# Pairwise outer products with batch norm: longer store runs and a rebuilt head, on one core

## Chip, cores, metric

The kernel runs on one core of one Trainium2 chip. The metric is the device time of one execution in microseconds, median of several.

## The reference

```python
# xi, xj: (1024, 39, 16); rows, cols: the 741 pairs r > c of 39 fields; W: (1, 16, 16)
cross = xj[:, rows, :, None] * xi[:, cols, None, :]
mean = jnp.mean(cross, axis=(0, 2, 3), keepdims=True)
var = jnp.mean(jnp.square(cross - mean), axis=(0, 2, 3), keepdims=True)
normed = (cross - mean) * jax.lax.rsqrt(var + 1e-5)
normed = normed * gamma[None, :, None, None] + beta[None, :, None, None]
out = normed[:, :, None, :, :] * W[None, None, :, :, :]      # 1024 x 1 x 741 x 16 x 16, fp32
```

The output is 777 MB, the inputs 5 MB. The mean and variance of each pair come from small moments of xi and xj (the head); then the kernel makes the output tile by tile. A tile is one row r (its r columns, each 256 numbers or 1 KB) for two of the eight batch indices t of each partition.

## The kernel before

```python
T = 2
WHOLE, LONG = 19, 28              # rows in one piece, in two; longer in four
FIRST_PIECES = (0, 3, 9, 19)
POOL_I, POOL_SHARE = 4, 0.13
ROW_GROUPS = ((19, 20), (15, 19), (20, 25), (25, 32), (1, 15), (32, 39))
# ... cut: pools, tiles, views
    half = T * (F - 1)
    mid = (F - 1) // 2
    tiles = [(mid, t0, t0 // T * half // 2) for t0 in range(0, NT, T)]
    slot = 0
    for r in range(mid + 1, F):
        for t0 in range(0, NT, T):
            tiles.append((r, t0, slot * half))
            if r < F - 1:
                tiles.append((F - 1 - r, t0, slot * half + T * r))
            slot ^= 1
# ... cut
    def products(n):              # every i fills all columns of the tile for one t
        xs = xs_of.pop(n)
        for t in range(T):
            for i in range(E):
                product(n, nc.scalar if i < E - POOL_I else nc.gpsimd, t, i, xs[:, t])

    def store(n, c0, c1):
        r, t0, _ = tiles[n]
        n0 = first[r]

        step = 1 if r > LONG and c1 == r else T
        for t in range(0, T, step):
            nc.sync.dma_start(
                out_v[:, t0 + t : t0 + t + step, (n0 + c0) * EE : (n0 + c1) * EE],
                view(n)[:, t : t + step, c0:c1, :].rearrange("p t n e -> p t (n e)"),
            )
# ... cut: affine, weigh (tiles 0 and 1)
    def bounds(r):
        if r <= WHOLE:
            return (0, r)
        if r <= LONG:
            return (0, r // 2, r)
        return (0, r // 5, r // 2, r - r // 5, r)

    def finish(n):

        r = tiles[n][0]
        n0 = first[r]
        y = view(n)
        split = r - int(r * POOL_SHARE + 0.5)
        for c in range(split, r):
            nc.gpsimd.tensor_scalar(
                y[:, :, c, :], y[:, :, c, :], t_sb[:, n0 + c : n0 + c + 1], 1.0, ALU.add, ALU.mult
            )
        if split < r:
            nc.gpsimd.tensor_tensor(
                y[:, :, split:r, :],
                y[:, :, split:r, :],
                w_sb.unsqueeze(1).to_broadcast([P, T, r - split, EE]),
                ALU.mult,
            )
        for c0, c1 in zip(bounds(r), bounds(r)[1:]):
            for c in range(c0, min(c1, split)):
                stt(
                    y[:, :, c, :],
                    y[:, :, c, :],
                    t_sb[:, n0 + c : n0 + c + 1],
                    w_dve.to_broadcast([P, T, EE]),
                    ALU.add,
                    ALU.mult,
                )
            store(n, c0, c1)
# ... cut: loads (x in four pieces of two t; W from GpSimd, gamma and beta into scratch),
#     then the statistics on two t at a time
        raw0 = raw_products(0, nc.scalar, range(32))
        raw1 = raw_products(1, nc.scalar, range(20))
        sums(0)
        emit(raw0, 8)
        nc.scalar.copy(w_dve, w_sb)
        for t in range(T):
            nc.tensor.matmul(
                ps_s[:, 0 : 2 * F], ones, total[:, t], start=t == 0, stop=t == T - 1
            )
        for t in range(T):
            nc.tensor.matmul(
                ps_r[0:F, 0:1], total[:, t, 0:F], ones[:, 0:1], start=t == 0, stop=t == T - 1
            )
# ... cut: shift, deviations (GpSimd), squares (ACT), moments and means (DVE), gram (PE)
        for to, acc in zip((g1, g2, g3), ps_g):
            nc.scalar.activation(to, acc[0:F, 0 : 2 * F + 1], AF.Copy, scale=1.0 / NB)
# ... cut: 14 DVE operations from these copies to var, all in SBUF; reciprocal, root on ACT,
#     five more operations to scale and shift (stq)
        def spread(r0, r1):
            n0, n1 = first[r0], first[r1 - 1] + r1 - 1
            ps = psx.tile([P, 512], F32, tag="ps", name="ps")
            ps_v = ps[:, 0 : 2 * (n1 - n0)].rearrange("p (x n) -> p x n", x=2)
            for r in range(r0, r1):
                nc.tensor.matmul(
                    ps_v[:, :, first[r] - n0 : first[r] - n0 + r],
                    pick[:, r, :],
                    stq[:, :, 0:r],
                    start=True,
                    stop=True,
                )
            nc.vector.tensor_tensor(
                st_sb[:, :, n0:n1],
                ps_v,
                gb_all[:, 0:1, n0:n1].to_broadcast([P, 2, n1 - n0]),
                ALU.mult,
            )
            nc.vector.tensor_add(st_sb[:, 1, n0:n1], st_sb[:, 1, n0:n1], gb_all[:, 1, n0:n1])

        spread(*ROW_GROUPS[0])
        affine(0)
        weigh(0, FIRST_PIECES)
        scale_xi(2)
        spread(*ROW_GROUPS[1])
        spread(*ROW_GROUPS[2])
        affine(1)
        weigh(1, bounds(tiles[1][0]))
        for group in ROW_GROUPS[3:]:
            spread(*group)

        for n in range(1, len(tiles)):
            if n == 1:
                products(2)
                scale_xi(3)
                continue
            if n + 2 < len(tiles):
                scale_xi(n + 2)
            finish(n)
            if n + 1 < len(tiles):
                products(n + 1)
```

Rows r and 38 - r form a pair that fills one half of the output buffer; the two halves alternate. ACT and GpSimd (POOL) make the products of a tile, DVE (and POOL for the last 13% of the columns) adds the shift and multiplies by W, SP issues the stores.

Terms used below. A *piece* is the part of a row's columns that leaves as one run for each batch index; a *packet* is what one of the 16 DMA engines moves at a time, here one run. A store *lands* when its last packet is written; the *lag* is how much later that is than the time at which as many bytes had left on average. A *hole* is time in which DMA engines stand idle, averaged over the 16 unless the text says that all rest. *Two pairs* is the time in which two pairs of rows are stored, some 47 us: the *loop through the buffer*, from the products of a tile to the landing that frees its place, has to fit into it. In the head, *raw products* are those of tiles 0 and 1, made before the statistics are known; the *affine* then applies scale and shift to them, *weighing* multiplies by W, and *spreading* copies the row factors (scale and shift of each pair) to all partitions by PE.

Of the kernel before, what the change touches and what calls it, by code (L numbers as in the profile page):

```python
# [7 lines left out]
F32 = mybir.dt.float32  # L8
# [4 lines left out]
BN_EPS = 1e-5  # L13
# [3 lines left out]

WHOLE = 19
LONG = 28
FIRST_PIECES = (0, 3, 9, 19)  # L20

POOL_I = 4
POOL_SHARE = 0.13

ROW_GROUPS = ((19, 20), (15, 19), (20, 25), (25, 32), (1, 15), (32, 39))


@with_exitstack
def tile_pair_outer_batchnorm(
# [40 lines left out]
    psp = ctx.enter_context(tc.tile_pool(name="ps", bufs=1, space=bass.MemoryType.PSUM))  # L70
    psx = ctx.enter_context(tc.tile_pool(name="psx", bufs=2, space=bass.MemoryType.PSUM))
    xi_sb = cpool.tile([P, NT, F, E], F32, name="xi_sb")
# [34 lines left out]
    pick = scratch("rest", F, F, P)  # L107
    gb_all = scratch("rest", P, 2, NP)
    total = scratch("rest", P, NT, 2 * F)
# [3 lines left out]
    shift_r = scratch("rest", F, 1)  # L113
    g1, g2, g3 = (scratch("rest", F, 2 * F + 1) for _ in range(3))
    k, mean, q1, q2, var, rstd, inv = (scratch("rest", F, F) for _ in range(7))
    stq = scratch("rest", F, 2, F)
    ps_s = psp.tile([P, 512], F32, name="ps_s")
    ps_r = psp.tile([P, 512], F32, name="ps_r")
    ps_g = [psp.tile([P, 512], F32, name=f"ps_g{n}") for n in range(3)]
    stt = nc.vector.scalar_tensor_tensor  # L120
# [39 lines left out]
    def products(n):  # L160

        xs = xs_of.pop(n)
        for t in range(T):
            for i in range(E):
                product(n, nc.scalar if i < E - POOL_I else nc.gpsimd, t, i, xs[:, t])

    def store(n, c0, c1):
        r, t0, _ = tiles[n]
        n0 = first[r]

        step = 1 if r > LONG and c1 == r else T
        for t in range(0, T, step):
            nc.sync.dma_start(  # L173
                out_v[:, t0 + t : t0 + t + step, (n0 + c0) * EE : (n0 + c1) * EE],
                view(n)[:, t : t + step, c0:c1, :].rearrange("p t n e -> p t (n e)"),
            )
# [27 lines left out]
    def bounds(r):  # L204
        if r <= WHOLE:
            return (0, r)
        if r <= LONG:
            return (0, r // 2, r)
        return (0, r // 5, r // 2, r - r // 5, r)

# [29 lines left out]
    with tc.manual_schedule():  # L240
        for t0 in range(0, NT, T):
            nc.sync.dma_start(xj_sb[:, t0 : t0 + T], xj_v[:, t0 : t0 + T])
            nc.scalar.dma_start(xi_sb[:, t0 : t0 + T], xi_v[:, t0 : t0 + T])
        nc.gpsimd.dma_start(w_sb[:, 0, :], w.rearrange("o i j -> (o i j)").partition_broadcast(P))
        nc.sync.dma_start(gb_all[:, 0], gamma.partition_broadcast(P))
        nc.scalar.dma_start(gb_all[:, 1], beta.partition_broadcast(P))
        nc.gpsimd.memset(ones, 1.0)
        nc.gpsimd.memset(fb[:, :, 2 * F : 2 * F + 1], 1.0)

# [8 lines left out]

        k_s = 1.0 / (T * P * E)
        batches = range(0, NT, T)  # L260
        sources = (xj_sb, xi_sb)
# [3 lines left out]

        def sums(t0):
            for x in range(2):
                nc.vector.tensor_reduce(  # L268
                    total[:, t0 : t0 + T, part(x)], sources[x][:, t0 : t0 + T], AX.X, ALU.add
                )  # L270
# [10 lines left out]
        def square(n):  # L281

            nc.scalar.activation(devs[n % 7], devs[n % 7], AF.Square, scale=0.25)  # L283

# [6 lines left out]
        def means(n):  # L291
            t0, x = n // 2 * T, n % 2
            to = fb if x else fa
            stt(  # L294
                to[:, t0 : t0 + T, 0:F],
                total[:, t0 : t0 + T, part(x)],
                1.0 / E,
                ps_u[:, x : x + 1, :].to_broadcast([P, T, F]),
                ALU.mult,
                ALU.subtract,  # L300
            )
# [8 lines left out]
        raw0 = raw_products(0, nc.scalar, range(32))  # L310
        raw1 = raw_products(1, nc.scalar, range(20))
        sums(0)
        emit(raw0, 8)
        nc.scalar.copy(w_dve, w_sb)
        for t in range(T):
            nc.tensor.matmul(
                ps_s[:, 0 : 2 * F], ones, total[:, t], start=t == 0, stop=t == T - 1
            )
        for t in range(T):
            nc.tensor.matmul(  # L320
                ps_r[0:F, 0:1], total[:, t, 0:F], ones[:, 0:1], start=t == 0, stop=t == T - 1
            )

        nc.scalar.activation(
            shift.rearrange("p x f -> p (x f)"), ps_s[:, 0 : 2 * F], AF.Copy, scale=k_s
        )
        nc.scalar.activation(shift_r, ps_r[0:F, 0:1], AF.Copy, scale=k_s)  # L327
        ps_u = ps_s[:, 2 * F : 4 * F].rearrange("p (x f) -> p x f", x=2)
        nc.scalar.copy(ps_u, shift)
        sums(2)  # L330
        for n in range(7):
            deviation(n)
        for n in range(2 * NT // T):
            square(n)
            emit(raw0, 3)
            if n % 2 == 1 and n < 5:
                sums(n + 3)
            moments(n)
            if n == 0:
                deviation(7)  # L340
            means(n)
            if n % 2 == 1:
                gram(n // 2 * T)
        emit(raw_products(1, nc.gpsimd, range(20, 32)), 12)
        emit(raw1, 6)

# [3 lines left out]

        for to, acc in zip((g1, g2, g3), ps_g):
            nc.scalar.activation(to, acc[0:F, 0 : 2 * F + 1], AF.Copy, scale=1.0 / NB)
        e_ab, e_abb, e_a = g1[:, 0:F], g1[:, F : 2 * F], g1[:, 2 * F : 2 * F + 1]
        e_aab, e_aabb, e_aa = g2[:, 0:F], g2[:, F : 2 * F], g2[:, 2 * F : 2 * F + 1]
        e_b, e_bb = g3[:, 0:F], g3[:, F : 2 * F]
        u, v = shift_r, shift[0:F, 1, :]
        emit(raw1, 6)

        stt(q2, e_ab, u, e_aab, ALU.mult, ALU.add)
        stt(k, e_b, u, e_ab, ALU.mult, ALU.add)  # L360
        nc.vector.tensor_scalar_mul(q2, q2, 2.0)
        stt(k, v, e_a, k, ALU.mult, ALU.add)
        stt(q2, v, e_aa, q2, ALU.mult, ALU.add)
        stt(q1, e_bb, u, e_abb, ALU.mult, ALU.add)
        nc.vector.tensor_mul(q2, q2, v)
        nc.vector.tensor_add(q1, q1, e_abb)
        stt(mean, v, u, k, ALU.mult, ALU.add)
        stt(q1, q1, u, e_aabb, ALU.mult, ALU.add)
        nc.vector.tensor_mul(k, k, k)
        nc.vector.tensor_add(q1, q1, q2)  # L370
        nc.vector.tensor_sub(q1, q1, k)
        nc.vector.tensor_scalar(var, q1, 0.0, BN_EPS, ALU.max, ALU.add)


        nc.vector.reciprocal(inv, var)
        nc.scalar.activation(rstd, inv, AF.Sqrt)
        emit(raw1, 8)
        nc.vector.tensor_mul(inv, var, rstd)
        nc.vector.tensor_mul(inv, inv, rstd)
        nc.vector.tensor_scalar(inv, inv, -0.5, 1.5, ALU.mult, ALU.add)  # L380
        nc.vector.tensor_mul(stq[:, 0], rstd, inv)
        stt(stq[:, 1], mean, -1.0, stq[:, 0], ALU.mult, ALU.mult)



        def spread(r0, r1):
            n0, n1 = first[r0], first[r1 - 1] + r1 - 1
            ps = psx.tile([P, 512], F32, tag="ps", name="ps")
            ps_v = ps[:, 0 : 2 * (n1 - n0)].rearrange("p (x n) -> p x n", x=2)
            for r in range(r0, r1):  # L390
                nc.tensor.matmul(  # L391
                    ps_v[:, :, first[r] - n0 : first[r] - n0 + r],
                    pick[:, r, :],
                    stq[:, :, 0:r],
                    start=True,
                    stop=True,
                )
            nc.vector.tensor_tensor(  # L398
                st_sb[:, :, n0:n1],
                ps_v,  # L400
                gb_all[:, 0:1, n0:n1].to_broadcast([P, 2, n1 - n0]),
                ALU.mult,
            )
            nc.vector.tensor_add(st_sb[:, 1, n0:n1], st_sb[:, 1, n0:n1], gb_all[:, 1, n0:n1])  # L404

        spread(*ROW_GROUPS[0])
        affine(0)
        weigh(0, FIRST_PIECES)
        scale_xi(2)
        spread(*ROW_GROUPS[1])  # L410
        spread(*ROW_GROUPS[2])
        affine(1)
        weigh(1, bounds(tiles[1][0]))
        for group in ROW_GROUPS[3:]:
            spread(*group)

        for n in range(1, len(tiles)):
# [4 lines left out]
            if n + 2 < len(tiles):  # L422
                scale_xi(n + 2)
            finish(n)
            if n + 1 < len(tiles):
                products(n + 1)
# [28 lines left out]
```

## Time and profile before

| | before |
|---|---|
| time | 1924.4 us |
| output written | 777 MB, 407 GB/s over the span |
| busy: DVE, ACT, POOL | 90%, 87%, 80% |
| packets on the store queue | 85,680 |
| first store issued, loop's DVE work begins | 49.4 us, 76.6 us |

A busy share of 90% on DVE does not make DVE the bound: the line of DMA shares, shown in the prediction, is full from 100 us on. Two more views carry the rest. First the store queue of the page: packets, MB, and the time its packets took as a share of 16 engines' span. Then three lines of the head's timeline: start and duration in us, engine, line, operation, what it writes and reads, count, and in brackets the idle time before it and what ended that.

```profile
q1 hardware_dynamic: 85680, 779.95, 97.3%
```

```profile
11.68 1.45 DVE L268 TENSOR_REDUCE y_sb<-xj_sb 128x78 f32<-128x1248 f32 x1 [1.50 <-DMA xj_sb<-in_r_xj_dram]
...
13.33 2.32 POOL L274 TENSOR_TENSOR y_sb<-xj_sb,y_sb 128x1248 f32<-128x1248 f32 x1 [6.34 <-ACT y_sb L327]
...
34.11 1.45 DVE L289 TENSOR_REDUCE y_sb<-y_sb 128x78 f32<-128x1248 f32 x1 [0.85 <-ACT y_sb L283]
```

The second load (t = 2, 3) is in at 11.7 us, the deviations on POOL begin at 13.3, and the last moment starts at 34.1.

### The profile page before, as it was taken

What the parts mean: (1) busy time and instruction counts of PE and PEld (TensorE: products, weight loads), DVE (VectorE), ACT (ScalarE), POOL (GpSimd) and SP (SyncE); (2) the same over time, 40 slices, a digit from 0 to 9 for tenths busy, and PEclk for the clock granted to TensorE, in tenths of its full rate; (3) what the DMA queues carried; (4) which work ended last, traced back from release to release, by engine and by line L of the source; (5) the groups of instructions that cost most, each with busy time, mean ns of one, the idle gap of its engine ahead of it and who ended that gap; (6) DMA issues with size and microseconds to landing.
All of it is one profiled execution on the core that took longest, in us unless ns stands there. A gap on an engine that the chain in (4) does not pass through costs nothing. (4 is left out here: it accounts for less than half of the span.)

```text
span 1923.2 us, 10490 instructions
## 1 busy us (share of the span) xinstructions
PE 25.5 (1%) x132; PEld 23.8 (1%) x132; DVE 1733.6 (90%) x2602; ACT 1663.9 (87%) x3690; POOL 1534.1 (80%) x1918
## 2 busy tenths in 40 slices
PE   2200000000000000000000000000000000000000
PEld 2200000000000000000000000000000000000000
DVE  5999989898989898999999998889898899898886
ACT  7998989898988988898898888888888888888762
POOL 6787878787878788888888888878887878777872
DMA  3699999999999999999999999999999999999999
GB/s 125 273 425 423 425 425 424 424 425 425 424 425 423 424 425 426 423 424 424 423 418 419 417 418 418 418 417 416 411 412 413 415 412 412 412 410 412 412 412 391
DMA packets 86529, 783.69 MB, mean 408 GB/s; under 512 B 5776, under 2 KB 6800, under 8 KB 35248
## 3 DMA queue, kind: packets, MB, share of 16 engines
q1 hardware_dynamic: 85680, 779.95, 97.3%
q10 hardware_dynamic: 720, 2.94, 0.4%
q14 instruction: 80, 0.66, 0.1%
q0 software_dynamic: 48, 0.13, 0.1%
q8 instruction: 1, 0.02, 0.0%
HBM read 6.00 MB, written 776.99 MB: 407 GB/s over the span
## 5 line engine op out<-in xcount | busy, mean ns | idle before, releaser
L230 DVE SCALAR_TENSOR_TENSOR y_sb<-y_sb,st_sb,w_dve 128x512 f32<-128x512 f32 x2542 | 1679.3, 741 | 154.5 <-issue 154.5
L132 ACT ACTIVATE y_sb<-xs,xj_sb 128x256 f32<-128x256 f32 (+33 forms) x3600 | 1613.9, 541 | 214.5 <-DMA out_dram<-y_sb 163.6
L134 POOL TENSOR_SCALAR y_sb<-xs,xj_sb 128x256 f32<-128x256 f32 (+33 forms) x1200 | 606.4, 529 | 22.8 <-DMA out_dram<-y_sb 22.7
L222 POOL TENSOR_TENSOR y_sb<-y_sb,w_sb 128x1024 f32<-128x1024 f32 (+4 forms) x138 | 442.3, 3205 | 11.5
L152 POOL TENSOR_TENSOR xs<-xi_sb,st_sb 128x576 f32<-128x576 f32 (+37 forms) x150 | 188.1, 1254 | 297.1 <-ACT y_sb L132 285.1
L218 POOL TENSOR_SCALAR y_sb<-y_sb,st_sb 128x512 f32<-128x512 f32 x384 | 260.5, 695 | 17.1 <-ACT y_sb L132 17.1
L132 ACT ACTIVATE y_sb<-xi_sb,xj_sb 128x304 f32<-128x304 f32 x52 | 23.9, 534 | 0.0
L196 DVE TENSOR_TENSOR y_sb<-y_sb,w_dve 128x1536 f32<-128x1536 f32 (+3 forms) x4 | 20.9, 5219 | 3.2 <-ACT y_sb L186 3.2
L188 POOL TENSOR_SCALAR y_sb<-y_sb,st_sb 128x512 f32<-128x512 f32 x18 | 13.6, 772 | 7.5 <-DVE st_sb L404 7.5
L391 PE MATMUL ps<-y_sb 39*128 39x38 f32 (+37 forms) x76 | 16.9, 398 | 20.1 <-DVE st_sb L398 13.9
L391 PEld LDWEIGHTS ps<-y_sb 39*128 39x128 f32 x76 | 16.4, 328 | 20.7 <-DVE st_sb L398 14.2
L289 DVE TENSOR_REDUCE y_sb<-y_sb 128x78 f32<-128x1248 f32 x8 | 11.6, 1448 | 3.5 <-ACT y_sb L283 3.3
L274 POOL TENSOR_TENSOR y_sb<-xj_sb,y_sb 128x1248 f32<-128x1248 f32 x4 | 9.3, 2326 | 6.3 <-ACT y_sb L327 6.3
L186 ACT ACTIVATE y_sb<-y_sb,st_sb 128x512 f32<-128x512 f32 x20 | 14.2, 800 | 0.0
L268 DVE TENSOR_REDUCE y_sb<-xj_sb 128x78 f32<-128x1248 f32 x4 | 5.8, 1450 | 8.9 <-DMA xj_sb<-in_r_xj_dram 8.9
L283 ACT ACTIVATE y_sb<-y_sb 128x1248 f32<-128x1248 f32 x8 | 9.8, 1229 | 2.2 <-POOL y_sb L274 2.2
L274 POOL TENSOR_TENSOR y_sb<-xi_sb,y_sb 128x1248 f32<-128x1248 f32 x4 | 9.3, 2324 | 0.0
L132 ACT ACT_TABLE_LOAD x1 | 1.3, 1283 | 7.9 <-DMA xi_sb<-in_r_xi_dram 7.9
L306 PE MATMUL ps_g<-y_sb 128*39 128x79 f32 x48 | 7.2, 339 | 18.6 <-DVE y_sb L294 18.6
L306 PEld LDWEIGHTS ps_g<-y_sb 128*39 128x39 f32 x48 | 6.1, 183 | 19.5 <-POOL y_sb L274 11.2
L134 POOL TENSOR_SCALAR y_sb<-xi_sb,xj_sb 128x304 f32<-128x304 f32 x12 | 6.0, 519 | 0.0
L268 DVE TENSOR_REDUCE y_sb<-xi_sb 128x78 f32<-128x1248 f32 x4 | 5.8, 1442 | 0.0
(42 smaller groups left out, 25.1 us busy)
## 6 DMA issues: line engine op xcount, KB each, us to landing
out_dram<-y_sb SPq DMA_DIRECT2D x48, 2816.0 KB, 12.9
out_dram<-y_sb SPq DMA_DIRECT2D x41, 2560.0 KB, 14.9
out_dram<-y_sb SPq DMA_DIRECT2D x32, 3072.0 KB, 17.3
out_dram<-y_sb SPq DMA_DIRECT2D x20, 3328.0 KB, 17.9
out_dram<-y_sb SPq DMA_DIRECT2D x16, 3584.0 KB, 17.8
out_dram<-y_sb SPq DMA_DIRECT2D x20, 2304.0 KB, 16.0
out_dram<-y_sb SPq DMA_DIRECT2D x25, 1536.0 KB, 15.0
out_dram<-y_sb SPq DMA_DIRECT2D x20, 1792.0 KB, 11.0
```

Source lines behind the costliest of these rows:

```text
L132: nc.scalar.activation(y, src, AF.Copy, scale=scale)
L134: engine.tensor_scalar(y, src, scale, 1.0, ALU.mult, ALU.mult)
L152: nc.gpsimd.tensor_tensor(xs, xi_sb[:, t0 : t0 + T, 0:r, :], s_sb[:, :, n0 : n0 + r, :].to_broadcast([P, T, r, E]), ALU.mult,)
L186: nc.scalar.activation(y[:, :, c, :], y[:, :, c, :], AF.Identity, bias=t_c, scale=s_c)
L188: nc.gpsimd.tensor_scalar(y[:, :, c, :], y[:, :, c, :], s_c, t_c, ALU.mult, ALU.add)
L196: nc.vector.tensor_tensor(y[:, :, c0:c1, :], y[:, :, c0:c1, :], w_dve.unsqueeze(1).to_broadcast([P, T, c1 - c0, EE]), ALU.mult,)
L218: nc.gpsimd.tensor_scalar(y[:, :, c, :], y[:, :, c, :], t_sb[:, n0 + c : n0 + c + 1], 1.0, ALU.add, ALU.mult)
L222: nc.gpsimd.tensor_tensor(y[:, :, split:r, :], y[:, :, split:r, :], w_sb.unsqueeze(1).to_broadcast([P, T, r - split, EE]), ALU.mult,)
L230: stt(y[:, :, c, :], y[:, :, c, :], t_sb[:, n0 + c : n0 + c + 1], w_dve.to_broadcast([P, T, EE]), ALU.add, ALU.mult,)
L274: nc.gpsimd.tensor_tensor(devs[n % 7], sources[x][:, t0 : t0 + T], shift[:, x : x + 1, :].unsqueeze(3).to_broadcast([P, T, F, E]), ALU.sub ...
L306: nc.tensor.matmul(acc[0:F, 0 : 2 * F + 1], lhs, fb[:, t], start=t == 0, stop=t == NT - 1)
L391: nc.tensor.matmul(ps_v[:, :, first[r] - n0 : first[r] - n0 + r], pick[:, r, :], stq[:, :, 0:r], start=True, stop=True,)
```

## The change

Its intent is twofold. The stores leave in fewer, longer runs: rows to 24 whole, to 31 in halves, longer in thirds. And the head, in which hardly anything is stored, is made shorter: smaller first loads, no second table load, small terms in PSUM (so that POOL can make 24 raw products meanwhile, instead of 12), gamma and beta loaded to where they are used, all row factors spread by PE at once and half of them applied only in the loop. The diff, cut to its core:

```diff
-WHOLE = 19
-LONG = 28
-FIRST_PIECES = (0, 3, 9, 19)
-POOL_I = 4
+ONE, TWO = 24, 31
+FIRST_PIECES = ((0, 2, 8, 19), (0, 9, 19))
+POOL_I, POOL_I_LONG = 4, 5
+LOADS = (0, 1, 2, 4, 8)
-ROW_GROUPS = ((19, 20), (15, 19), (20, 25), (25, 32), (1, 15), (32, 39))
+ROW_GROUPS = (     # rows, PSUM bank, tile after which the group is applied
+    (19, 20, 0, None), (15, 19, 1, None), (20, 25, 1, None), (1, 15, 2, 8), (25, 32, 3, 16), (32, 39, 4, 24)
+)
 ...
+        split = E - (POOL_I_LONG if tiles[n][0] > TWO else POOL_I)     # in products
-        step = 1 if r > LONG and c1 == r else T                        # in store
+        step = 1 if r > ONE and c1 == r else T
     def bounds(r):
-        if r <= WHOLE:
-            return (0, r)
-        if r <= LONG:
-            return (0, r // 2, r)
-        return (0, r // 5, r // 2, r - r // 5, r)
+        pieces = 1 + (r > ONE) + (r > TWO)
+        return tuple(q * r // pieces for q in range(pieces + 1))
 ...
-        nc.gpsimd.dma_start(w_sb[:, 0, :], w.rearrange("o i j -> (o i j)").partition_broadcast(P))
-        nc.sync.dma_start(gb_all[:, 0], gamma.partition_broadcast(P))
-        nc.scalar.dma_start(gb_all[:, 1], beta.partition_broadcast(P))
+        nc.sync.dma_start(st_sb[:, 0], gamma.partition_broadcast(P))
+        nc.sync.dma_start(st_sb[:, 1], beta.partition_broadcast(P))
+        nc.sync.dma_start(w_sb[:, 0, :], w.rearrange("o i j -> (o i j)").partition_broadcast(P))
 ...
-        sums(0)
-        emit(raw0, 8)                       # raw products on ACT
-        nc.scalar.copy(w_dve, w_sb)
-        ... means from t = 0, 1
+        nc.scalar.activation(shift_r, ones[0:F, 0:1], AF.Sqrt)      # loads the table early
+        sums(0, 1)
+        ... means from t = 0 alone
 ...
-        u, v = shift_r, shift[0:F, 1, :]
-        stt(q2, e_ab, u, e_aab, ALU.mult, ALU.add)
-        stt(k, e_b, u, e_ab, ALU.mult, ALU.add)
-        nc.vector.tensor_scalar_mul(q2, q2, 2.0)
-        ... 14 operations, all in SBUF
+        p_v, p_v_half, p_q1, p_q2, p_mean, p_var, p_newton = (cell(n) for n in range(7))   # PSUM
+        stt(k, p_b, u, e_ab, ALU.mult, ALU.add)
+        stt(q2, e_ab, u, p_aab, ALU.mult, ALU.add)
+        stt(k, p_v, e_a, k, ALU.mult, ALU.add)
+        ... 12 operations, one input of each in PSUM where it can be
 ...
-        spread(*ROW_GROUPS[0]) ... five more times, each matmuls and two DVE operations
+        all matmuls of all groups at once, into five banks
+        def apply(group):
+            ps, n0, n1 = spread_of[group]
+            nc.vector.tensor_mul(ps[:, 1], ps[:, 1], st_sb[:, 0, n0:n1])
+            nc.vector.tensor_mul(st_sb[:, 0, n0:n1], ps[:, 0], st_sb[:, 0, n0:n1])
+            nc.vector.tensor_add(st_sb[:, 1, n0:n1], ps[:, 1], st_sb[:, 1, n0:n1])
+        # groups 0 to 2 before the loop, 3 to 5 in it, after tiles 8, 16 and 24
```

## The prediction

> **What bounds the kernel now.** I read the 40 slices of the page first, then a table of windows, the timeline of the head, and the waits of the store queue.
>
> ```profile
> DMA  3699999999999999999999999999999999999999
> GB/s 125 273 425 423 425 425 424 424 425 425 424 425 423 424 425 426 423 424 424 423 418 419 417 418 418 418 417 416 411 412 413 415 412 412 412 410 412 412 412 391
> ```
>
> From the third slice on the DMA engines are full, so the stores bound the kernel although DVE (90%), ACT (87%) and POOL (80%) look busier. Two things can shorten it: the two thin slices at the start, and a higher rate afterwards. The rate has steps, 425, 418, 412. The windows lie inside the stretches with 2, 3, 5 and 5 pieces per pair of rows (r and 38-r):
>
> ```profile
> 90.00:111.00 21.00, 0.00 (x0) 0.00 (x0) 21.00 (x33) 20.54 (x47) 18.92 (x25) 1.00 1.01 430
> 300.00:900.00 600.00, 0.00 (x0) 0.00 (x0) 552.16 (x837) 539.24 (x1217) 494.38 (x634) 1.00 1.01 424
> 965.00:1230.00 265.00, 0.00 (x0) 0.00 (x0) 241.63 (x367) 234.28 (x530) 216.51 (x278) 1.00 1.01 418
> 1320.00:1790.00 470.00, 0.00 (x0) 0.00 (x0) 423.11 (x641) 413.92 (x930) 375.48 (x473) 1.00 1.00 412
> ```
>
> The last two columns are DMA share and GB/s. The short first window counts packets by their start; prorated, its packets moved 427.4 GB/s. So a pair of rows moves at 427.4, 424.0 and 417.3 GB/s when cut in 2, 3 and 5 pieces. The head, with the store queue's first issues:
>
> ```profile
> 37.93 0.46 ACT L352 ACTIVATE y_sb<-ps_g 39x79 f32<-39x79 f32 x3
> ...
> 41.04 1.28 ACT L376 ACT_TABLE_LOAD   x1
> ...
> 47.59 1.75 DVE L196 TENSOR_TENSOR y_sb<-y_sb,w_dve 128x1536 f32<-128x1536 f32 x1 [2.70 <-ACT y_sb L186]
> 49.37 83.02 SPq L173 DMA_DIRECT2D out_dram<-y_sb  x11
> ...
> 60.52 10.28 DVE L196 TENSOR_TENSOR y_sb<-y_sb,w_dve 128x9728 f32<-128x9728 f32 x1
> ...
> 75.34 1.30 DVE L404 TENSOR_TENSOR st_sb<-st_sb,y_sb 128x245 f32<-128x245 f32 x1
> ...
> 76.56 58.67 DVE L230 SCALAR_TENSOR_TENSOR y_sb<-y_sb,st_sb,w_dve 128x512 f32<-128x512 f32 x89
> ```
>
> The first store leaves at 49.4 us; then DVE is the bound: tile 1 is weighed from 60.5 to 70.8, six us of spreading follow, and the loop's DVE work starts at 76.56. The packets show four holes after the first store (52.3, 57.8, 65.9 and 83.4 us, 14.7 us together); from 88.96 us on no hole is left until 1300. So **the full stream begins at 88.96 us**, one tile of DVE work after 76.56.
>
> Third reading: the landing of each store against the time at which that many bytes had left on average. The lag is 0.4 us at 50, 4.1 at 908, 5.3 at 1262, and falls back to 0.4 at 1850. After 1300 the packets show some 16 small holes (10 us, averaged over engines), in which two engines still work; all 16 rest together for only 1.4 us after 1800. So **a slower engine or two set the end**: their pace is 422.1 GB/s at 3 pieces and 415.6 at 5, and holes in the others cost nothing. The slow ones may be those that fetch the 80 packets of instructions; that is not shown.
>
> **What the Trainium skill says.** "DMA: Bandwidth & Descriptors", Specifications, gives a fabric ceiling of 435 GB/s and an HBM limit of about 358 per core. The trace writes 424 for 600 us: the first agrees, the second does not hold here. The same page, Issuing engines are not separate DMA queues: moving beta and W to the SP queue changes no bandwidth. "ScalarE: Activation LUTs", What ACT_TABLE_LOAD costs: about 1283 ns, here 1.28 us, twice. "SBUF — State Buffer", on the shared port pair: a DVE instruction with two SBUF inputs contends with a GpSimd instruction that reads SBUF. That is why terms go to PSUM while POOL does more raw products; in the trace of before POOL rests in that stretch, so no run shows it yet.
>
> **The change, part by part.**
>
> *Pieces.* Rows 20 to 24 lose one piece each, 29 to 31 two, 32 to 38 one: 5 + 6 + 7 = 18. A piece is 1024 runs, 64 packets per engine: 1152 packets fewer per engine. One packet's price: a pair is 38,912 bytes per partition and batch; times 16 it takes 1456.7 ns at 427.4, 1468.4 at 424.0 and 1492.0 at 417.3, so 11.7 ns for one packet more and 23.6 for two. **1152 x 11.8 ns = 13.6 us less.** Runs of 20 to 24 KB are new; I assume that they follow the line.
>
> *Can whole stores still be fed?* The tightest loop is row 24, where the same half of the buffer is written again after two pairs: ACT 24 x 0.50 = 11.9 us, DVE 21 columns x 0.66 = 13.9, issue to data 1.2, transfer 14.7, landing 3.8 of which 3.4 is lag: 45.6 against two pairs at 46.6. It fits, and the slow engine has 3.4 us more. For row 38 in thirds with 11 of 16 parts on ACT: DVE to the second third 16.5, 1.2, its transfer 7.9, half of the last 4.1, landing 3.8, ACT 15.4: 48.9 against 47, but 45.5 for the slow engine. So only fast engines rest, and the 1.4 us in which all rested go.
>
> *Head.* The first loads are half as long: both inputs of t=0 at about 6.0 instead of 7.4 us. ACT no longer sits in raw products when the sums arrive, so the deviations on POOL can start near 8.9 instead of 13.3. Eight of them (2.28 each) then end at 27, and DVE becomes the bound: from 11.7 (the load of t=2,3) six sums and eight moments of 1.45 and six means of 0.17 give 33.1, against 35.7 before. Gram 1.8: 34.9 (before 37.56). The terms: copies to 35.5, then five raw products (2.3) stand ahead of the square of k on ACT, so DVE waits until 38.0; reciprocal to 38.9, root 0.2 without a table load to 39.1, five operations to 40.2 (before 43.7). Spread and three DVE operations to 41.7. ACT still has raw products to 42.7, so its affine starts at 42.7 instead of 46.0, and POOL's at 41.8. The first piece (2 columns) is weighed by 44.7: **first store 44.8 instead of 49.4.** Second piece 49.0, third (11 columns, 6.0) 55.9; six operations for rows 15 to 24, 1.7; tile 1, 10.4 in two pieces: 68.0. ACT has tile 2's products at 67.6. The spreads of the longer groups are out of the way, so the loop starts at **68.0 instead of 76.56**. Tile 2 takes 17 x 0.66 = 11.2 there: store at 79.3, data at **80.2 instead of 88.96: 8.7 us.** Tile 3 is ready at 91.4 while tile 2 is still leaving (to 91.9), row 20 whole at 102.7 against 103.5: no hole, but margins under 1 us.
>
> *Sum.* Stream of before from 88.96 to the last packet at 1921.9: 1833.0. Less 13.6 and 1.4: 1818.0. From 80.2 it ends at 1898.2; 1.3 to the end of the span, 1.2 from the span to the timed run: **1900.7, say 1900 us**, 1.3% less.
>
> **Rivals.**
> (a) *The mean engine sets the end*: then the 10 us of holes after 1300 come back too, and the time is some 1892. Against it: two engines work through those holes. For it: in before the lag is gone by 1800, so part of the holes may bind.
> (b) *Whole stores starve the queue*: the row 24 loop has 1 us to spare on the fast engines, and the first whole row starts with a thin backlog. Holes of 3 us in each of the 20 pairs with rows 20 to 24 would take 60 us, and 1950 would come out; I think a few us at most, since stores of before stand 14 to 18 us in the queue there.
> (c) *The rate is capped near 425*: then rows 20 to 24 give nothing, 5 of the 18 pieces, and it is 1904. The 427.4 of the whole 19-column runs speaks against it.
> (d) *The head gains less*: three PSUM operations per group, ACT in raw products ahead of the square, POOL with 24 raw products to 39. Each can cost 1 to 3 us: 1903.
>
> **Range and chances.** Most weight lies on 1897 to 1904; (a) sets the low end, 1890, (d) with small holes the high end, 1910. More than 2% faster means under 1886: that would need (a) and a head 6 us better than mine, 0.06. Slower by over 2% needs heavy starvation, 0.01. Same 0.93.
>
> **What would show it.** First store near 45 us, the loop's DVE work at 68, the last early hole closed near 80. Windows of rows 20 to 24 at 427, 25 to 31 still 424, 32 to 37 near 420. No table load after the first. The lag of landings growing to about 8 us by the end and not falling back. I am wrong if holes appear in the first 500 us (b), if the lag stays small and the end comes below 1893 (a), or if 20 to 24 stay at 424 (c).

## The result, and the profile after

| | before | after |
|---|---|---|
| time, median of 6 | 1924.37 us | 1895.8 us |
| ratio | | 0.9851 (0.9838 to 0.9863) |
| first store issued | 49.4 us | 41.3 us |
| loop's DVE work begins | 76.56 us | 63.94 us |
| full stream begins | 88.96 us | 76.35 us |
| from there to the last packet | 1833.0 us | 1816.4 us |

The change makes the kernel 1.5% faster, 28.6 us: by the two traces **12.6 us in the head and 16.6 in the stream**. On a scale that calls under 2% "same", this is "same", as forecast; the interval of the ratio lies clear of 1. The page of the changed kernel, DMA share and GB/s in 40 slices, and its store queue:

```profile
DMA  3899999999999999999999999999999999999999
GB/s 147 362 426 430 425 430 426 427 428 422 430 424 425 424 425 425 424 426 424 423 426 424 425 424 422 424 421 421 421 421 421 418 414 420 414 418 417 417 418 389
...
q1 hardware_dynamic: 66912, 780.46, 97.9%
```

18,768 packets fewer than before, in nearly the same bytes. By the traces 18,176 of them are packets of output, 1136 for each of the 16 engines: the predicted 1152, less 16 because tile 1 now leaves in two pieces. The rate now reads 427 or so where it was 425, stays at 424 where it fell to 418, and 421 and then 414 to 420 where it was 412. The windows over rows 20 to 23, 25 to 28, 29 to 31 and above (DMA share and GB/s are the last two columns):

```profile
105.00:460.00 355.00, 0.00 (x0) 0.00 (x0) 333.99 (x512) 322.18 (x729) 294.67 (x378) 1.00 1.00 428
...
570.00:930.00 360.00, 0.00 (x0) 0.00 (x0) 330.54 (x502) 324.78 (x734) 294.68 (x379) 1.00 1.01 425
...
960.00:1230.00 270.00, 0.00 (x0) 0.00 (x0) 249.85 (x380) 239.88 (x540) 225.88 (x294) 1.00 1.01 424
1250.00:1790.00 540.00, 0.00 (x0) 0.00 (x0) 491.27 (x744) 448.09 (x1027) 469.88 (x597) 1.00 1.00 419
```

Rows 25 to 28, whose pieces did not change, kept their rate; rows 20 to 23 and 29 to 31 rose by the steps that one and two pieces fewer make. Above 31 one piece fewer would make some 3 GB/s; the rest of the 7 is that the fast engines' holes, which began near 1350 us before, now begin at 1514. The head's timeline:

```profile
3.07 1.28 ACT L318 ACT_TABLE_LOAD   x1 [3.07 <-issue]
...
7.60 2.32 POOL L278 TENSOR_TENSOR y_sb<-xj_sb,y_sb 128x1248 f32<-128x1248 f32 x1 [1.89 <-ACT y_sb L322]
...
9.09 1.46 DVE L272 TENSOR_REDUCE y_sb<-xj_sb 128x78 f32<-128x1248 f32 x1 [0.62 <-DMA xj_sb<-in_r_xj_dram]
...
23.88 5.52 DVE L294 TENSOR_REDUCE y_sb<-y_sb 128x78 f32<-128x1248 f32 x4
...
31.73 0.20 ACT L367 COPY y_sb<-ps 39x79 f32<-39x79 f32 x1
...
40.00 1.22 DVE L202 TENSOR_TENSOR y_sb<-y_sb,w_dve 128x1024 f32<-128x1024 f32 x1 [2.14 <-ACT y_sb L192]
41.25 67.40 SPq L179 DMA_DIRECT2D out_dram<-y_sb  x9
...
53.62 10.34 DVE L202 TENSOR_TENSOR y_sb<-y_sb,w_dve 128x4608 f32<-128x4608 f32 x2
...
63.94 51.44 DVE L233 SCALAR_TENSOR_TENSOR y_sb<-y_sb,st_sb,w_dve 128x512 f32<-128x512 f32 x78
```

The deviations begin 5.7 us earlier than before, the moments end at 29.4 instead of 35.6, and the loop follows directly on tile 1 (53.62 + 10.34 = 63.96), where six microseconds of spreading stood before. There is one table load, at 3 us, and no other.

### The profile page after: what moved, and what is told of

Read it like the earlier page. It is cut to its first block, busy times and chain, and to the rows that moved or that the text cites. A ratio compares the mean times of both kernels' runs of the same rounds, so it can differ in the third digit from the quotient of the medians.

```text
span 1894.1 us, 10252 instructions
## 1 busy us (share of the span) xinstructions
PE 24.5 (1%) x128; PEld 23.1 (1%) x128; DVE 1730.9 (91%) x2609; ACT 1621.5 (86%) x3625; POOL 1574.5 (83%) x1985
## 5 line engine op out<-in xcount | busy, mean ns | idle before, releaser
L137 ACT ACTIVATE y_sb<-xs,xj_sb 128x256 f32<-128x256 f32 (+32 forms) x3544 | 1576.5, 537 | 228.4 <-DMA out_dram<-y_sb 170.3
L139 POOL TENSOR_SCALAR y_sb<-xs,xj_sb 128x560 f32<-128x560 f32 (+35 forms) x1256 | 643.0, 534 | 39.4 <-DMA out_dram<-y_sb 31.1
L225 POOL TENSOR_TENSOR y_sb<-y_sb,w_sb 128x1024 f32<-128x1024 f32 (+4 forms) x138 | 441.9, 3202 | 11.5
L202 DVE TENSOR_TENSOR y_sb<-y_sb,w_dve 128x1024 f32<-128x1024 f32 (+4 forms) x5 | 20.9, 4205 | 3.9 <-ACT y_sb L192 3.9
L137 ACT ACTIVATE y_sb<-xi_sb,xj_sb 128x304 f32<-128x304 f32 x40 | 18.7, 534 | 0.1
L194 POOL TENSOR_SCALAR y_sb<-y_sb,st_sb 128x512 f32<-128x512 f32 x18 | 13.5, 766 | 0.3 <-issue 0.3
L139 POOL TENSOR_SCALAR y_sb<-xi_sb,xj_sb 128x304 f32<-128x304 f32 x24 | 11.9, 528 | 0.0
L294 DVE TENSOR_REDUCE y_sb<-y_sb 128x78 f32<-128x1248 f32 x8 | 11.1, 1443 | 0.0
L272 DVE TENSOR_REDUCE y_sb<-xj_sb 128x78 f32<-128x1248 f32 (+1 forms) x5 | 5.9, 1189 | 5.5 <-DMA xj_sb<-in_r_xj_dram 5.5
L311 PE MATMUL ps<-y_sb 128*39 128x79 f32 x48 | 7.2, 339 | 16.6 <-DVE y_sb L294 16.6
L311 PEld LDWEIGHTS ps<-y_sb 128*39 128x39 f32 x48 | 6.1, 183 | 17.5 <-DVE y_sb L294 9.6
L272 DVE TENSOR_REDUCE y_sb<-xi_sb 128x78 f32<-128x1248 f32 (+1 forms) x5 | 5.9, 1186 | 0.1
L254 POOL TENSOR_SCALAR_AFFINE_SELECT y_sb<-y_sb 39x4992 f32<-39x4992 f32 x1 | 4.6, 4624 | 0.0
(45 smaller groups left out, 16.9 us busy)
```

Of the source, the lines that this page charges most:

```text
L137: nc.scalar.activation(y, src, AF.Copy, scale=scale)
L139: engine.tensor_scalar(y, src, scale, 1.0, ALU.mult, ALU.mult)
L194: nc.gpsimd.tensor_scalar(y[:, :, c, :], y[:, :, c, :], s_c, t_c, ALU.mult, ALU.add)
L202: nc.vector.tensor_tensor(y[:, :, c0:c1, :], y[:, :, c0:c1, :], w_dve.unsqueeze(1).to_broadcast([P, T, c1 - c0, EE]), ALU.mult,)
L225: nc.gpsimd.tensor_tensor(y[:, :, split:r, :], y[:, :, split:r, :], w_sb.unsqueeze(1).to_broadcast([P, T, r - split, EE]), ALU.mult,)
L311: nc.tensor.matmul(acc[0:F, 0 : 2 * F + 1], lhs, fb[:, t], start=t == 0, stop=t == NT - 1)
```

## The experiments

Each run is compared with runs of the kernel before on the same chip in the same rounds; "gain" is the difference of the two medians. The changed kernel's gain is 28.6 us. The medians of the kernel before lie between 1924.4 and 1924.8 in the four sets of rounds, so half a microsecond is noise. Every result agreed with the reference.

| run | what it is | time | gain |
|---|---|---|---|
| e1 | pieces alone | 1907.94 | 16.9 |
| e2 | head alone | 1913.14 | 11.7 |
| e3 | change, W loaded first, by GpSimd | 1896.93 | 27.9 |
| e4 | change, whole rows to 31, halves above | 1903.15 | 21.6 |
| e5 | change, terms in SBUF | 1898.47 | 26.1 |
| e6 | change, all groups applied before the loop | 1898.60 | 26.0 |
| e7 | change, no early table load | 1895.77 | 28.8 |
| e8 | change, every row whole | 2068.79 | -144.2 |
| e9 | change, 9664 useless PE instructions | 1915.59 | 8.9 |
| e10 | change, whole to 28, halves above | 1890.58 | 33.9 |
| e11 | change, four of 16 products on POOL throughout | 1896.39 | 28.1 |
| e12 | e10, five of 16 products on POOL above 24 | 1889.41 | 35.3 |

### The two halves of the change (e1, e2)

e1 is the kernel before with the new `bounds`, `step` and `POOL_I_LONG`; e2 is the changed kernel with the old ones:

```diff
-        pieces = 1 + (r > ONE) + (r > TWO)                    # e2
-        return tuple(q * r // pieces for q in range(pieces + 1))
+        (bounds, step rule and POOL_I of before)
```

> The kernel before with the change's pieces alone (whole to row 24, halves to 31, thirds above, the last piece split by t, five of 16 products on POOL above row 31); the head stays as before. Theory: the stream of before, 1833.0 us from 88.96 to the last packet, loses 1152 packets x 11.8 ns = 13.6 us and the 1.4 us in which all engines rested, so 1924.4 - 15.0 = 1909.4 us; the difference of the two traces from the start of the full stream on (1833.0 to 1816.4, 16.6 us) says 1907.8. Rival, packets' cost is hidden by a cap near 425 GB/s: rows 20 to 24 give nothing, 1913. Rival, the mean engine sets the end: 24 us less, 1900.

> The changed kernel with the pieces of before (19, 28, quarters above; four of 16 products on POOL throughout): the head alone. Theory: the full stream starts at 76.35 instead of 88.96 us and nothing else differs, so 1924.4 - 12.6 = 1911.8 us, and the lag of the landings again rises to about 5 us near 1260 and is gone by 1850. Rival, an earlier stream is given back later through longer holes: above 1915.

Measured: 1907.9 and 1913.1. The gains add up, 16.85 + 11.65 = 28.5 against 28.6, so the parts do not disturb each other within the noise. e1 falls on the value that the traces' difference gave, 2 us below the sum of packets and holes (15.0), and is far from the cap (1913) and the mean engine (1900). e2 gave back 1 us of its 12.6: its trace has 3.7 us after 1800 in which all engines rest together, 1.4 in the kernel before.

### Where the head was faster than predicted (e3)

```diff
-        nc.sync.dma_start(w_sb[:, 0, :], w...partition_broadcast(P))    # after the other loads
+        nc.gpsimd.dma_start(w_sb[:, 0, :], w...partition_broadcast(P))  # ahead of everything on POOL
```

> The changed kernel with one thing undone in the loads: W goes out first and from the GpSimd queue, as before. Theory: W's 48 packets of 4 KB, which took 0.16 to 1.2 us each before, are what delayed the second and third loads; the load of t=2,3 lands at about 11.7 us again instead of 9.1, DVE's sums start there, and everything to the loop moves by 2.6 us: the loop's DVE work at 66.5 instead of 63.9 and 1898.4 us instead of 1895.8. Rival: it is the smaller first loads and the later beta, W does not matter: 1895.8 and t=2,3 at 9.1.

Measured: 1896.93, 0.7 us of gain lost, and the loop's DVE work at 65.07, 1.1 us later. The load of t = 1 lands at 8.2 instead of 6.2 us and that of t = 2, 3 at 11.1 instead of 9.1: W in front (32 packets of 4 KB, the other 16 carry 4 bytes) does hold the loads up by 2 us, most of the 2.6 by which the prediction had this load too late. Only 1.1 reaches the loop: DVE's first term starts 1.98 us after it fell idle instead of 2.57, because in the changed kernel ACT is still busy with eight raw products when the sums are ready (its copy starts at 31.73, PE ended at 31.3), and here it is not.

### Three details of the head (e5, e6, e7)

```diff
-            return ps_c[0:F, 64 + n * F : 64 + (n + 1) * F]            # e5: eight terms
+            return terms[n]                                           # in SBUF scratch
-        # e6: groups 3 to 5 after tiles 8, 16, 24
+        for group in range(3, 6): apply(group)                        # before the loop
-        nc.scalar.activation(shift_r, ones[0:F, 0:1], AF.Sqrt)         # e7: left out
```

> The changed kernel with its eight small terms in SBUF instead of PSUM, all else the same. POOL makes raw products from 25.8 to 37.7 us, over the whole chain of DVE (31.97 to 36.6). Theory, from the skill's page on SBUF: a DVE instruction with two SBUF inputs waits for a GpSimd instruction that reads SBUF, 0.5 us each; 10 of the 17 DVE instructions of the chain then have two SBUF tensor inputs, each waits for a quarter to a half us, so the chain takes 3 to 5 us longer and the time is 1899 to 1901 us. Rival: operands of 39x39 are too short for that to matter: chain 4.6 us and 1896 as now.

Measured: 1898.5, 2.5 us lost, a little less than expected. One instruction carries most of it; the timeline of e5 and, below it, the same instruction of the changed kernel:

```profile
32.50 2.16 DVE L378 SCALAR_TENSOR_TENSOR y_sb<-y_sb 39x39 f32<-39x39 f32 x1
34.59 0.58 DVE L379 SCALAR_TENSOR_TENSOR y_sb<-y_sb 39x39 f32<-39x39 f32 x1
```

```profile
32.31 0.24 DVE L377 SCALAR_TENSOR_TENSOR y_sb<-ps,y_sb 39x39 f32<-39x39 f32 x1
32.48 0.24 DVE L378 SCALAR_TENSOR_TENSOR y_sb<-ps,y_sb 39x39 f32<-39x39 f32 x1
```

With both inputs in SBUF it takes 2.16 us instead of 0.24 while POOL reads SBUF; after POOL's raw products end (38.0) such instructions take 0.19 again. Not all are slowed alike: L382 of e5 has two SBUF inputs too and took 0.18. The Trainium skill ("SBUF — State Buffer", Who interferes with whom, on the shared port pair) says that a DVE instruction with two SBUF inputs contends with a GpSimd instruction that reads SBUF; this run shows it, and the terms in PSUM save these 2.5 us while POOL makes its 24 raw products there.

> The changed kernel with the three late groups of row factors applied before the loop, where the kernel before had them, instead of after tiles 8, 16 and 24. Theory: nine DVE instructions of 105 to 245 columns, some 3 to 4 us, stand again between tile 1 and the loop, the full stream starts that much later, and the time is 1899 us. Rival: DVE is not the bound there: 1895.8.

Measured: 1898.6, 2.6 us lost. Nine DVE instructions take the time from 63.6 to 66.3 between tile 1 and the loop, and the loop begins at 66.31. DVE is the bound of this stretch.

> The changed kernel without the early square root that loads the table at 3 us: a second table load of 1.28 us is then made ahead of the square root in the chain. Theory: the spread, and all to the loop, move by 1.3 us: 1897.1 us. Rival: ACT's raw products fill the time, and the affine on ACT (39.1) hides part: under 0.5 us.

Measured: 1895.8, nothing lost; the rival was right. The second table load is there, 34.10 to 35.39, but it starts before the reciprocal on DVE (34.56) and ends just after it: DVE goes on at 35.66 instead of 35.47, and it had started its terms 0.2 us earlier. The 0.4 us that the chain loses do not reach the stores: ACT's affine comes after its own raw products, at 39.04 against 39.10. In the kernel before, ACT's raw products kept the table load until 41.04, after the reciprocal. There an earlier load may have been worth more; no run shows that.

These runs do not cover the whole head. By the two timelines its 12.6 us are 6.3 up to the first term (38.30 to 31.97), 0.8 in the chain of terms and 5.5 from there to the loop. The order of W (e3) isolates 1.1 of the first part, the late groups (e6) 2.6 of the last. The smaller first loads, the reordered raw products and the spreading of all groups at once, to which the rest falls, were not tested one by one.

### How long the runs may be (e4, e8, e10, e11, e12)

```diff
-        pieces = 1 + (r > ONE) + (r > TWO)
+        pieces = 1 + (r > 31)       # e4;  1 in e8, with step = T;  1 + (r > 28) in e10 and e12
-POOL_I, POOL_I_LONG = 4, 5
+POOL_I, POOL_I_LONG = 4, 4          # e11;  in e12 five from row 25 on
```

> The changed kernel with every row stored whole, in one store for both t: 1344 packets per engine fewer than now, worth 15.9 us by the price per packet alone, 1879.9. But by the loop (ACT's products, 0.66 us of DVE for each column it does, 1.8 to data, the transfer) rows from 28 on no longer fit into two pairs, 47 us: row 31 needs 52.6, row 34 56, row 38 62. Theory: the sum of what is over, two loops for each row, is 172 us: about 2050 us, with holes in all engines growing from row 28 on and none before. Rival, the queue of stores is deep enough to cover it: 1880 to 1900.

Measured: 2068.8, 144 us slower than the kernel before; the loop sum gave 2050. The slices of e8:

```profile
DMA  4899999999999999999999888888887898777778
GB/s 157 377 429 427 428 426 430 426 426 423 425 425 417 430 417 417 413 412 397 395 388 386 378 366 377 366 365 370 348 343 333 341 386 352 329 307 334 304 303 386
```

The rate falls from about 900 us on, where row 28 begins to be late, to 303; from there on all 16 engines rest together for 164 us. In that stretch DVE stands idle for 11.5 us before its tile at 1634.6, and ACT waits for landings, here in row 35:

```profile
1620.06 19.86 ACT L137 ACTIVATE y_sb<-xs,xj_sb 128x560 f32<-128x560 f32 x46 [13.49 <-DMA out_dram<-y_sb]
```

> The changed kernel with longer runs still: whole rows to 31 (above 24 as two stores, one for each t, which adds no packets), halves above. 14 pieces fewer, 896 packets per engine. Theory, price per packet and the slowest engine never starved: 10.6 us less, 1885.2. The loop through the buffer at row 31, whole: 17.8 of DVE, 1.8 to data, 18.9 of transfer, half of ACT's products 7.1, that is 45.6 us against 46.9 for two pairs. Rival, whole stores starve the queue because the lag of 5 us counts in this loop: 50 against 46.9, 3 us in each of the loops from row 28 on, some 20 us lost: 1905.

Measured: 1903.2, 7 us slower than the change: near the rival's number, but not for its reason. Within a row little is lost (three holes of 0.4 to 0.5 us); the others stand at the changes of row, 94 to 98 us apart, and from 850 on they grow: 0.7 us at 566, 1.6 at 850, 2.8 at 944, 4.4 at 1041, 6.6 at 1139. A tile's t = 0 and t = 1 lie one behind the other, so when a row grows by one column, the first half of the new tile needs the first column of the old second half, which lands last. The timeline of e4 at the change to row 31, before the largest hole:

```profile
1112.43 21.18 ACT L137 ACTIVATE y_sb<-xs,xj_sb 128x496 f32<-128x496 f32 x48 [10.11 <-DMA out_dram<-y_sb]
1127.01 21.82 DVE L233 SCALAR_TENSOR_TENSOR y_sb<-y_sb,st_sb,w_dve 128x512 f32<-128x512 f32 x33 [9.80 <-issue]
```

The old row's store of t = 0 landed at 1102.9, that of t = 1 at 1112.3, and only then ACT begins; the new row's first store is issued at 1145.0, when the engines have been idle since about 1139. My loop for this run had left that out. At the change to row 32 ACT waits as long (9.9 us), but row 32 leaves in halves, its first store comes earlier, and no hole follows. A column to spare between the tiles might remove the wait; no run tried it.

> The changed kernel with rows 25 to 28 whole too (as two stores, one for each t) and halves from 29 on: 11 pieces fewer, 704 packets per engine, 8.3 us by the price per packet. The run with whole rows to 31 lost 13 us in which all engines rested, nearly all at the changes from row 29 to 30 and 30 to 31, where the first column of the new row lies on the last column in t=0 that the old row's second store still holds. Worked out for such a change (0.6 after that landing, ACT's products, DVE, 1.2 to data, against the two pairs in between): row 28 is 0.5 us late, row 29 2 us, row 30 3.7, row 31 5.5. Theory: with whole rows to 28 only, nothing that counts is lost: 1888 us, faster than both kernels. Rival: every row change from 25 on costs the slowest engine a microsecond: 1892.

Measured: 1890.6, between theory and rival, and 5.3 us better than the change instead of 8.3. (Of e4's 13.5 us with all engines at rest, 9.5 lie at the changes to rows 30 and 31, so "nearly all" was too much.) The holes at the changes to rows 25 to 28 are 0.7, 0.9, 1.0 and 1.6 us; the lag of the landings, by which the slowest engine stays busy through such holes, falls from 1.6 to about 0.5 there, and in 1.2 us all engines rest.

> The version with whole rows to 28 and halves above, with five of 16 products on POOL from row 25 on instead of from row 32 on. At a row change of that version the new row starts late because ACT's products begin only when the old row's second store has landed; two of 24 products fewer on ACT make that 1.1 us shorter. Theory: the holes of all engines at the changes to rows 27 and 28 (some 1.2 us) and most of the 3 us that that version missed of its own estimate go: 1888 to 1889 us. Rival: POOL, at 83% there, then comes last with its ten products, and nothing is won or some lost: 1890.6 or more.

Measured: 1889.4, a gain of 35.3 us against 33.9 for e10. All engines rest 0.4 us there instead of 1.2. **This is the fastest version found, 1.85% faster than the kernel before** (ratio 0.9815, 0.9799 to 0.9832) and 0.3% faster than the change.

> The changed kernel with four of 16 products on POOL in the rows above 31 too, as before. Theory: the loop through the buffer gets 1.3 us longer in rows 32 to 38, still within two pairs for the slowest engine, so the fast engines rest more after 1500 and the time moves by less than 1 us: 1896 to 1897. Rival, ACT is what holds the last rows: row 38 loses 1 to 2 us in each of its loops and the time is 1899 or more.

Measured: 1896.4, 0.5 us lost. The fast engines' holes begin near 1460 instead of 1514, and the end hardly moves: the fifth product on POOL is worth no more than the noise in the changed kernel.

### What the lag of the landings is (e9)

```diff
         for n in range(1, len(tiles)):
+            for _ in range(16):
+                nc.tensor.matmul(banks[0][0:F, 0:1], w_sb[:, 0, 0:F], w_sb[:, 0, F : F + 1], start=True, stop=True)
```

> The changed kernel with 2416 useless matmuls on the idle PE (W into an unused bank; they wait for nothing in the loop), 9664 instructions, which doubles the instructions to be fetched: some 75 more packets of 8 KB on the instruction queue, at 0.32 us 24 us of one DMA engine. Theory A, an engine's instructions are fetched through one DMA engine, and the lag of the landings is the fetching of ACT's 3600 and DVE's 3000 instructions (28 and 24 packets, 9 and 8 us): then PE's DMA engine becomes the slowest, its lag reaches some 15 to 20 us, and the time is 1905 to 1915. Theory B, fetches are spread over all 16: 24/16, 1.5 us more, 1897, the lag stays below 6. Theory C, the lag is a slow engine's own and has nothing to do with fetches: as B in time, the lag unchanged.

Measured: 1915.6, 19.7 us of the gain lost, though PE has nothing to do with the output. PE runs through its instructions until about 378 us. The queues and the windows of e9, and two windows of the changed kernel over the same times:

```profile
q8 instruction: 39, 0.64, 0.1%
q14 instruction: 78, 0.64, 0.1%
```

```profile
150.00:250.00 100.00, 100.00 (x1503) 100.00 (x1503) 87.31 (x135) 83.63 (x190) 78.16 (x100) 1.00 0.97 407
250.00:350.00 100.00, 100.00 (x1503) 100.00 (x1503) 87.27 (x135) 82.84 (x188) 78.13 (x100) 1.00 0.94 394
```

```profile
150.00:250.00 100.00, 0.00 (x0) 0.00 (x0) 96.20 (x149) 91.65 (x209) 84.89 (x108) 1.00 1.01 429
250.00:350.00 100.00, 0.00 (x0) 0.00 (x0) 93.76 (x144) 88.30 (x201) 83.36 (x110) 1.00 1.00 426
```

PE's instructions come on a queue of their own, 39 packets of 16 KB instead of 1; the other queue keeps its 78. These 0.62 MB are 23 us of one engine at a sixteenth of 427 GB/s, and the time moves by 20: they are carried by one engine, or few. The lag of the landings rises from 0.6 us at 51 to 9.2 at 292; meanwhile the others rest (16 us of holes between 100 and 400 us, most of it with at most two engines at work) and wait for the slot that the late engine holds. After 392 us the lag is back at 2.4 or less and goes on much as in the changed kernel. Theory A stands, though its range was missed by 0.6 us and its lag, 15 to 20 us, was put too high. That ACT's and DVE's own 78 packets of 8 KB (0.31 us each, 24 us of engine time) make the lag of both kernels is what this suggests: if ACT's 3600 instructions, about 28 of the packets, use one engine, they take 8.7 us of it. But which engine carries which packet is not in the trace, so this is an estimate, not shown.

The packets of the kernel before say one thing more. Between 100 and 1270 us, where its lag grows to 5.7, 65 of 44,664 store packets took over 150 ns longer than the median of their size. All 65 started between 1.7 us before and 0.4 us after the start of one of the 50 instruction fetches in that time. So the long delays of single packets come with fetches; that an engine is also slower by a few ns on every packet (theory C) is not excluded, since 2 ns over its 2790 packets would make the same lag.

## Why the prediction was right

The prediction was 1900 us, within 1890 to 1910; measured 1895.8.

- **Price of a packet, 13.6 us.** Right in kind, a little small. e1 measures 16.9 for pieces and holes together, against 15.0. Of the 1.4 us of common rest that it counted, all went. The other 1.8 us are not traced to a cause; fewer stores and their semaphore packets (896 fewer in e1, 9 ns each, over 16 engines 0.5 us) may be a part. The durations of single packets, which the prediction did not use, agree with the price: a line through their means by size gives 11.2 ns (before) and 12.1 ns (after) for what does not grow with the size.
- **The rate is not capped at 425.** Runs of 20 to 24 KB follow the line: packets of 24,576 bytes took 919.5 ns, 921 by the line from the shorter ones. Rival (c) falls.
- **Whole stores to row 24 are fed.** Right: one hole (0.8 us at 472, the change to row 24). The arithmetic within a row held; what it lacked is the change of row, which e4 showed, and it was luck that the change stops at 24. Rival (b) comes true by degrees for whole rows above that (e10, e4), not here.
- **The head, 8.7 us.** Measured 12.6. These 3.9 us are most of the error of the sum, 4.9 us (1900.7 to 1895.8); the stream was 1.6 us shorter than summed, and the two small terms after the last packet 0.6 longer. The mis-sized term is "DVE becomes the bound: from 11.7 (the load of t=2,3) six sums and eight moments of 1.45": the load is in at 9.1, because W no longer goes first (2 us of it by e3), and the reductions follow each other every 1.38 us, not 1.45 (1.0 us over 14), as the trace of before already had it (starts at 7.37 and 8.74). From there on every step stands 3.5 to 4.1 us earlier than predicted: terms at 32.0, factors at 36.6, first store at 41.3, loop at 63.9 (68.0), full stream at 76.35 (80.2). Of the rival (d)'s costs, the contention is real (e5), and PSUM avoids it; ACT's raw products ahead of the copies cost some 0.6 us (e3).
- **A slower engine sets the end.** The stream took 1816.4 us against my 1818.0 for the slowest and 1809 for the mean engine; in the changed kernel the fast engines rest 6.5 us after 1500 and all 16 never together; e9 moved the end by slowing one engine. Rival (a) falls. Wrong is the detail that the lag would grow to 8 us and stay: it reached 5.9 near 1498 and fell to 0.3 at the end, as the loop of the longest rows lets the fast engines rest.
- **The table load.** Predicted as a saving of 1.3 us; e7 shows that its new place is worth nothing in this head.

## What to carry to other kernels

When the store stream is the bound, count packets: here each costs its engine 11.8 ns, whatever its size between 5 and 24 KB, and the time follows that count until a buffer can no longer be refilled within its turn. Work that turn out (landing, products, last operation, issue, transfer), and do it also for the place where the layout shifts, since the worst overlap there decides how long a run may be. And look for what the slowest DMA engine does besides the data: an idle engine's instructions are not free.

## What the Trainium skill lacked or had wrong

- No fault, though the prediction took it for one: the 358 GB/s of "DMA: Bandwidth & Descriptors", Specifications, is by the same page's section Measured what each core gets when both cores of an HBM domain stream. This core, the only one that ran the kernel, wrote 424 to 428 GB/s for hundreds of microseconds, near the page's fabric ceiling of 435.
- The same page prices packets for small transfers only; for long packets on stores the rates of 2, 3 and 5 pieces show 11.8 ns each, between 5 and 24 KB.
- "Runtime: NRT & Kernel Launch", Instruction fetch mechanics, says that fetching is hidden since it is faster than the issue. For the engine that issues it is; but 38 fetches of 16 KB for PE cost a kernel bound by its stores 19.7 us (e9), because they do not spread evenly over the 16 DMA engines. The page names blocks of 16 KiB; PE's packets have that size, those of the other queue 8 KB.
- No page sizes the lag between engines in a long stream ("DMA: Bandwidth & Descriptors" says that two of them are usually slower, without a figure): landings up to 5.7 us behind the mean in the kernel before (packets and landings of its trace), 9.2 in e9.
- "ScalarE: Activation LUTs", What ACT_TABLE_LOAD costs, has 1283 ns right (1.28 us here) and adds a drain of 1380 ns: no such gap is seen here (ACT's next instruction starts at 4.36 after the load of 3.07 to 4.35; in the kernel before the load at 41.04 follows raw products that end at 41.01), and a load that lies beside other waits cost no time that is clear of noise (e7).
